# Layer-1 source lists ranked forward, four of them cut before the last group, one set of operations a destination block

## The chip, the cores and the metric

The kernel runs on one core of one Trainium2 chip. Time is device time in microseconds (us), the median of several executions. TensorE is called PE in the profile, VectorE DVE, ScalarE ACT, GpSimd POOL, and SyncE, which starts plain transfers, SP. POOL starts the gathers (indirect transfers).

## The reference, cut to what matters

A graph of N = 2708 nodes with 256 features passes two layers, each followed by a residual sum and a normalisation.

```python
# layer 0: adj without its diagonal; three attention heads and two gated cells
x = layernorm(x + L0(x, adj))
# layer 1: attention over the edges with adj > 0.5, four heads of 64 channels
h = (x @ W).reshape(n, 4, 64)
e = leaky_relu(s_src[:, None, :] + s_dst[None, :, :], 0.2)
e = where((adj > 0.5)[:, :, None], e, -1e9)
alpha = softmax(e, axis=0)                        # over sources i
out = einsum('ijh,ihc->jhc', alpha, h).reshape(n, 256) + bias
x = layernorm(x + out)
```

The graph is sparse, and low-numbered nodes have many more edges than high-numbered ones.

## The kernel before, in words

**Tiling.** The nodes are 22 tiles of 128 (the last has 20 rows), in six groups of 512 destinations; group 5 has only tiles 20 and 21, 148 nodes. Layer 0 takes the groups in the order 4, 3, 2, 1, 0, 5 (`turn`, L423). A dense pass over the transposed adjacency comes first; it leaves, for each tile of sources and block of destinations, which sources have an edge, and the adjacency of layer 1 as bit words.

**Lists.** `listed(l, batch)` (L716) turns those flags into lists of source numbers for a batch of destination blocks of layer l. It runs over five engines in turn: DVE makes flags F and a scan C; PE multiplies them with constant matrices into ranks (`rk`, one PSUM bank); DVE adds positions (`pos`, one row for each span of tiles in `spans`, L519), rounds, and builds two one-hot arrays; PE multiplies them, 22 tiles in groups of four, into `lst` (one PSUM bank); ACT copies; PE transposes; DVE writes the indices (`f_idx1` for layer 1). Layer 1 has 32 blocks (`BLOCKS1`, L53: start, width, room in tiles of 128 sources), cut into five batches, `batch1`. Rooms do not depend on the data; a list is filled up to its room.

**Layer 0 by group.** `layer0` (L1074) sums gathered columns and rows on PE; `cells_and_norm` (L1130) computes attention, two gated cells (PE products, ACT sigmoid and tanh, DVE gate operations), the normalisation, and the rows of layer 1: into DRAM table T1 go 260 words of features and exponentials a node beside its adjacency bits, into X1 the normalised rows, into Sd the destinations' values. Its POOL part sums rows into `xacc` and adds a bias, eight adds a group of four tiles. Its last PE operation is the transpose of `f_dd`, by which a group's end is read below. The lists of layer 1 are written after the last group in the program (L1279).

**Layer 1.** `work1` (L1332) cuts each block's sources into steps of at most two tiles, 56 steps in all. `fetch_h` (L1344) gathers a step's rows of T1, 128 rows of 352 words in each gather, into one of five slots (`hg_ring`, two tiles each), up to four steps ahead (`ahead1` = 5). `layer1` (L1355) has three DVE operations a step, the triple: adjacency words to a mask, the maximum of destination values S and source values into q, and q times the mask. Then PE multiplies each tile's features with q, four heads a tile, into the block's accumulator; each is two instructions in the trace. When the last block of a tile of 128 destinations is complete, `finished(b)` (L1394) copies by ACT, transposes by PE, divides, adds X1 and normalises on DVE and ACT, and stores by SP. The values S of a group, 128 x 4 x 512, come by SP from Sd (`spread_values`). S, y and the transposition's input lie in arena `big`, from its start, one after the other (L1302); layer 0 uses the same bytes earlier.

**The order.** Almost every operation is recorded and not issued at once (so nearly all profile lines read L375, `Order.issue`). `spans` (L134) says which pieces of memory an operation touches, in cells of 32 bytes of a partition; from this come the dependencies. `duration` (L180) prices each operation. A list scheduler then goes forward and backward 12 times, takes the order with the shortest planned time and issues all engines' operations in it; each engine executes its own share in that order and waits only for what an operation depends on. A table `SOONER` (L85, empty) adds to the priority of all operations recorded under a named part in the first turn.

Of the kernel before, what the change touches and what calls it, by code (L numbers as in the profile page):

```python
# [84 lines left out]
SOONER = {}  # L85


class Order:
# [44 lines left out]
    @staticmethod  # L133
    def spans(ap):  # L134

        name, pat, wide = ap.tensor.name, [tuple(d) for d in ap.ap], _width(ap.dtype)
        if name.startswith("in_"):
            return name, []
        space = str(ap.space)
        if "PSUM" in space:  # L140
            return name, [(0, 1)]
        if "DRAM" in space:
            at, cell = ap.offset, 1024
        else:
            step = pat[0][0]
            at, cell = (ap.offset % step if step else ap.offset), 32
            pat = pat[1:]
        run, outer = 1, []
        for s, n in sorted((abs(s), n) for s, n in pat if s and n > 1):
            if s <= run + cell // wide:  # L150
                run = s * (n - 1) + run
            else:
                outer.append((s, n))
        starts = [at]
        for s, n in outer:
            starts = [a + k * s for a in starts for k in range(n)]
        out = []
        for a in sorted(starts):
            lo, hi = a * wide // cell, (a + run) * wide - 1
            hi = hi // cell + 1  # L160
            if out and lo <= out[-1][1]:
                out[-1] = (out[-1][0], max(hi, out[-1][1]))
            else:
                out.append((lo, hi))
        return name, out
# [234 lines left out]
def fast_path(ctx: ExitStack, tc: tile.TileContext, i: dict, out: bass.AP, bad: bass.AP):  # L400
# [22 lines left out]
    turn = [4, 3, 2, 1, 0, 5]  # L423
    ADD, SUB, MUL, MAX = ALU.add, ALU.subtract, ALU.mult, ALU.max
# [94 lines left out]
    spans = sorted({(b[2], NB) for b in BLOCKS0} | {(0, NB)})  # L519
# [3 lines left out]
    for n, (lo, hi) in enumerate(spans):  # L523
        V.tensor_scalar(pos[:, n], pos_i, float(-P * lo), None, op0=ADD)
        if lo:
            V.memset(pos[:, n, :lo], 1.0e6)
        V.tensor_add(pos[:, n, last:], pos[:, n, last:], past)
# [51 lines left out]
    batch1 = batches_of(BLOCKS1, [(0, N)])  # L579
    slot = ({}, {})  # L580
# [135 lines left out]
    def listed(l, batch):  # L716
# [11 lines left out]
        first = [blocks[k][2] if l == 0 else 0 for k in ns]  # L728
        for m, q in enumerate(first):
            if q:  # L730
                V.memset(F[:, m, :q], 0.0)
        V.tensor_tensor_scan(
# [22 lines left out]
        while m < n:  # L755
            e = m
            while e < n and first[e] == first[m]:
                e += 1
            V.tensor_add(
                r[:, m:e], ru[:, m:e],  # L760
                pos[:, spans.index((first[m], NB))].unsqueeze(1).to_broadcast([P, e - m, NB]),
            )
            m = e
# [22 lines left out]
        b_lo = min(first)  # L786
# [492 lines left out]
    for b in batch1:  # L1279
        listed(1, b)  # L1280
# [20 lines left out]
    big.reset()  # L1301
    S_ring = Ring([big.take([P, HEADS1, CH]) for _ in range(3)])  # L1302
    y_ring = Ring([big.take([P, D]) for _ in range(4)])
    o_ring = Ring([big.take([C65, HEADS1, P]) for _ in range(2)])
# [22 lines left out]
    hg_ring = Ring([lists.take([P, 2, TW1]) for _ in range(5)])  # L1327
    q_ring = Ring([lists.take([P, 2, HEADS1, P]) for _ in range(3)])
    mask_ring = Ring([lists.take([P, 2, 8, 16], U16) for _ in range(3)])
# [3 lines left out]
    for n, (d0, w, room_) in enumerate(BLOCKS1):  # L1333
        work1 += [(n, list(range(t, min(t + 2, room_)))) for t in range(0, room_, 2)]
# [9 lines left out]
    def fetch_h(j):  # L1344
        n, ts = work1[j]
        hg = hg_ring.next()
        for m, t in enumerate(ts):
            c = column[1][n] + t
            gathered(hg[:, m, :].bitcast(U32), T1, idx[1][:, c : c + 1], 0)
        hg_of[j] = hg  # L1350

    outs = {}
    x1b_of = {}

    def layer1(j):  # L1355
# [3 lines left out]
        nt, at = len(ts), d0 - base[d0 // CH]  # L1359
# [5 lines left out]
            mask, words.unsqueeze(3).to_broadcast([P, nt, nw, 16]) if nt > 1 else  # L1365
            words.unsqueeze(3).to_broadcast([P, nt, nw, 16]),
# [10 lines left out]
        if d0 % P == 0 and ts[0] == 0:  # L1377
            outs[b] = acc.next()
            x1b_of[b] = xb_ring.next()
            Q.dma_start(x1b_of[b][: size[b]], X1[b * P : b * P + size[b], :])  # L1380
        o = outs[b]
        p0 = d0 % P
        for m, t in enumerate(ts):
            with R.together():
                for h in range(HEADS1):
                    T.matmul(
                        o[:C65, h * P + p0 : h * P + p0 + w], lhsT=hg[:, m, h * C65 : (h + 1) * C65],
                        rhs=q[:, m, h, :], start=(p0 == 0 and t == 0 and h == 0), stop=(t == room_ - 1),
                        skip_group_check=True,
                    )  # L1390
        if ts[-1] == room_ - 1 and d0 + w == min((b + 1) * P, N):
            finished(b)

    def finished(b):  # L1394
# [6 lines left out]
        with R.together():  # L1401
# [6 lines left out]
        V.tensor_mul(  # L1408
            y.rearrange("p (h c) -> p h c", h=HEADS1), got[:, :, :C1], dn.unsqueeze(2).to_broadcast([p, HEADS1, C1])
        )  # L1410
# [9 lines left out]
    ahead1 = 5  # L1420
# [466 lines left out]
```

## Time and profile before

| what | us |
|---|---|
| median of three runs (lowest, highest) | 898.7 (895.02, 906.93) |
| profiled execution, its time | 901.63 |
| its span | 899.9 |
| PE busy, DVE busy | 678.9, 551.1 |
| POOL busy, ACT busy | 436.2, 233.0 |
| end of group 4, 3, 2 (last transpose of each) | 316.14, 420.00, 523.41 |
| end of group 1, 0, 5 | 615.03, 681.37, 712.44 |
| first gather of layer 1 starts | 714.55 |
| first DVE operation of layer 1 | 727.14 |

The mean granted PE clock is 0.851 of full speed. The profile is one execution, so its durations are compared with its own time; the median of the runs is 0.3% lower. Busy time is a sum over the whole span, in which different engines set the pace at different times; the ends of groups above show where one stage gives way to the next. In rows of groups, "idle before" names what ended the engine's wait.

### The profile page before, as it was taken

The page shows a single profiled execution, that of the slowest core. Times are in us where ns is not written, and L with a number is a line of the kernel's source. Part 1 is how long each engine was busy: PE and PEld are TensorE (multiplying, and loading weights), DVE is VectorE, ACT ScalarE, POOL GpSimd, SP SyncE. Part 2 cuts the span into 40 slices and gives each one's busy share as a digit, 9 for nine tenths or more (in the row PEclk, how much of TensorE's full clock was granted, in tenths as well). Part 3 has the DMA queues.
Part 4 walks back from the last instruction along what each step waited for, and adds up shares of the span by engine and source line. Part 5 has one row for each costly group of instructions (what it writes and reads, how often), then busy time and mean ns, then how long its engine had stood idle before and what let it go on. Part 6 is the DMA issues. An engine that isn't in the chain of part 4 may idle for free. (4 is left out here: it accounts for less than half of the span.)

```text
span 899.9 us, 12878 instructions
## 1 busy us (share of the span) xinstructions
PE 678.9 (75%) x4588; PEld 481.8 (54%) x4588; DVE 551.1 (61%) x1355; ACT 233.0 (26%) x496; POOL 436.2 (48%) x565
## 2 busy tenths in 40 slices
PE   1474764778769899988898879999988565776664
PEld 1463653565335555565555545564467464765553
DVE  7373576695126847763436644561498734977996
ACT  4403664001011321122111121123125301113244
POOL 7006000476725716666677777550005266777830
PEclk9995555588979999999999999999999855787886
DMA  9934886572101312243223222121004244555541
GB/s 300 335 124 144 280 307 186 164 227 59 23 17 47 120 57 51 44 113 84 51 53 91 81 74 74 51 74 42 1 1 130 106 124 124 175 154 169 159 139 47
DMA packets 60647, 103.50 MB, mean 115 GB/s; under 512 B 20887, under 2 KB 37027, under 8 KB 59935
## 3 DMA queue, kind: packets, MB, share of 16 engines
q1 hardware_dynamic: 40337, 61.41, 20.5%
q0 software_dynamic: 17472, 41.15, 17.6%
q8 instruction: 38, 0.62, 0.3%
q10 hardware_dynamic: 2766, 0.04, 0.2%
q14 instruction: 34, 0.28, 0.1%
HBM read 93.07 MB, written 12.27 MB: 117 GB/s over the span
## 5 line engine op out<-in xcount | busy, mean ns | idle before, releaser
L375 POOL DMA_INDIRECT f_raw<-in_adjT_dram,f_idx x115 | 116.2, 1011 | 47.7 <-issue 31.9
L375 PE MATMUL acc<-f_lists 128*65 128x128 f32 (+3 forms) x768 | 100.3, 303 | 51.7 <-DVE f_lists L375 37.9
L375 POOL DMA_INDIRECT f_lists<-f_T,f_idx x96 | 108.6, 1132 | 50.2 <-issue 20.6
L375 PE MATMUL side<-f_xT,f_wts 128*128 128x512 f32 (+1 forms) x288 | 123.0, 553 | 13.0 <-DVE f_big L375 11.9
L375 PE MATMUL side<-f_big,f_wts 128*128 128x512 f32 (+1 forms) x288 | 123.1, 553 | 9.5 <-ACT f_big L375 8.4
L375 PEld LDWEIGHTS acc<-f_lists 128*65 128x65 f32 x768 | 92.0, 189 | 58.4 <-DVE f_lists L375 42.6
L375 PEld LDWEIGHTS side<-f_big,f_wts 128*128 128x128 f32 x288 | 53.1, 194 | 64.4 <-issue 54.9
L375 POOL DMA_INDIRECT f_xg__133<-f_T,f_idx x36 | 39.1, 1085 | 99.5 <-DMA f_T<-f_E 71.6
L375 PEld LDWEIGHTS side<-f_xT,f_wts 128*128 128x128 f32 x288 | 51.0, 191 | 60.7 <-issue 43.3
L375 ACT ACTIVATE f_big<-f_wts 128x1024 fp8e4<-128x1024 f32 (+2 forms) x66 | 61.7, 952 | 48.3 <-DMA f_wts<-in_adjT_dram 39.8
L375 POOL TENSOR_TENSOR f_xacc<-f_xacc,f_low 128x256 f32<-128x256 f32 (+1 forms) x22 | 22.6, 1029 | 96.9 <-ACT f_low L375 96.1
L375 ACT ACTIVATE f_big<-side,f_biases 128x512 f32<-128x512 f32 (+1 forms) x48 | 30.4, 636 | 129.3 <-PE side L375 76.6
L375 DVE TENSOR_TENSOR f_big<-f_big 128x512 f32<-128x512 f32 (+1 forms) x48 | 30.4, 636 | 49.7 <-ACT f_big L375 42.8
L375 DVE TENSOR_SCALAR f_wts<-f_wts 128x1024 fp8e4<-128x1024 f32 (+1 forms) x66 | 43.2, 662 | 25.1 <-DMA f_wts<-in_adjT_dram 23.3
L375 PE MATMUL side<-f_big,f_gat_w 128*128 128x512 f32 (+1 forms) x144 | 56.1, 544 | 2.5 <-DVE f_s_d L375 1.6
L375 DVE TENSOR_TENSOR f_lists<-f_big,f_lists 128x512 f32<-128x512 f32 (+4 forms) x56 | 44.3, 791 | 21.3 <-PE acc L375 6.9
L375 PEld LDWEIGHTS <-f_big 128*128 128x128 fp8e4 x968 | 36.4, 103 | 34.2 <-issue 18.6
L375 POOL DMA_INDIRECT f_xg__135<-f_T,f_idx x33 | 34.7, 1052 | 36.9 <-PE acc L375 24.4
L375 PE MATMUL side<-f_pow,f_wts 128*128 128x8 bf16 x484 | 23.6, 170 | 37.1 <-DVE f_wts L375 35.6
L375 PEld LDWEIGHTS <-f_lists 128*32 128x32 f16 (+6 forms) x617 | 35.4, 134 | 27.1 <-DVE f_lists L375 17.2
L375 PE MATMUL lst<-f_lists 128*128 128x256 f16 (+4 forms) x285 | 37.5, 297 | 16.0 <-DVE f_lists L375 16.0
L375 DVE TENSOR_TENSOR f_lists<-f_iota,f_lists 128x2816 f16<-128x2816 f16 (+5 forms) x26 | 49.4, 1922 | 0.3
(244 smaller groups left out, 1208.2 us busy)
## 6 DMA issues: line engine op xcount, KB each, us to landing
f_wts<-in_adjT_dram SPq DMA_DIRECT2D x42, 512.0 KB
f_wts<-in_adjT_dram SPq DMA_DIRECT2D x21, 330.0 KB
f_big<-f_Rd SPq DMA_DIRECT2D x5, 1024.0 KB
f_big<-f_Sd SPq DMA_DIRECT2D x5, 1024.0 KB
f_T<-f_ah SPq DMA_DIRECT2D x21, 132.0 KB
f_X<-f_low SPq DMA_DIRECT2D x21, 128.0 KB
f_low<-f_X SPq DMA_DIRECT2D x21, 128.0 KB
out_dram<-f_big SPq DMA_DIRECT2D x21, 128.0 KB
```

The lines of the kernel that those rows point to most:

```text
L375: getattr(getattr(self.nc, engine_), method)(*args, **kw)
```

## The change

Lists: the batches of layer 1 are recorded as part `lists1`, which gets 300 more in the scheduler's first turn. For the first four blocks (`split1`, destinations 0 to 191) the lists hold only sources of tiles 0 to 19 (`SPLIT` = 20): the flags beyond are set to zero, positions come from a span (0, 20), and their gathers name T1's first 2560 rows only. The sources of tiles 20 and 21 are added as whole tiles: `hlast` is filled by two plain SP transfers and a POOL memset once, and each of the four blocks takes a further step over these two tiles, after the four blocks' listed steps.

Steps: a step holds up to five tiles, so one block is one step, but for the block of seven tiles (4 + 3); 37 steps in all. The ring of rows has three slots of five tiles, the masks have two slots, q has two slots in xT, whose columns 0 to 2559 layer 0 no longer reads once group 0 is done. Rows are fetched two steps ahead (`ahead1` = 3). Accumulation starts and stops by a count of steps left for a tile (`todo1`).

Places: S, y and the transposition's input get fixed places in `big`, each over a layer-0 buffer that is done with early. In `finished`, an even tile's division is four ACT operations in place of one DVE operation. The scheduler's cells are 16 bytes. Rooms, and so the number of gathers (96), are unchanged.

```diff
-SOONER = {}
+SOONER = {'lists1': 300}
...
             step = pat[0][0]
-            at, cell = (ap.offset % step if step else ap.offset), 32
+            at, cell = (ap.offset % step if step else ap.offset), 16
             pat = pat[1:]
...
     turn = [4, 3, 2, 1, 0, 5]
+    SPLIT = base[turn[-1]] // P
     ADD, SUB, MUL, MAX = ALU.add, ALU.subtract, ALU.mult, ALU.max
...
     G.iota(pos_i, pattern=[[P, NB]], base=0, channel_multiplier=1)
-    spans = sorted({(b[2], NB) for b in BLOCKS0} | {(0, NB)})
+    spans = sorted({(b[2], NB) for b in BLOCKS0} | {(0, NB), (0, SPLIT)})
     pos = home("f_pos", [P, len(spans), NB])
...
             V.memset(pos[:, n, :lo], 1.0e6)
-        V.tensor_add(pos[:, n, last:], pos[:, n, last:], past)
+        if hi < NB:
+            V.memset(pos[:, n, hi:], 1.0e6)
+        else:
+            V.tensor_add(pos[:, n, last:], pos[:, n, last:], past)
     ids = home("f_ids", [P, NB, NL], F16)
...
     batch1 = batches_of(BLOCKS1, [(0, N)])
+
+    split1 = range(4)
     slot = ({}, {})
...
         V.tensor_scalar(F, source[:, s0 : s0 + n, :], 0.0, None, op0=ALU.is_gt)
-        first = [blocks[k][2] if l == 0 else 0 for k in ns]
-        for m, q in enumerate(first):
+        reach = [(blocks[k][2], NB) if l == 0 else (0, SPLIT if k in split1 else NB) for k in ns]
+        for m, (q, e) in enumerate(reach):
             if q:
                 V.memset(F[:, m, :q], 0.0)
+            if e < NB:
+                V.memset(F[:, m, e:], 0.0)
         V.tensor_tensor_scan(
...
             e = m
-            while e < n and first[e] == first[m]:
+            while e < n and reach[e] == reach[m]:
                 e += 1
...
                 r[:, m:e], ru[:, m:e],
-                pos[:, spans.index((first[m], NB))].unsqueeze(1).to_broadcast([P, e - m, NB]),
+                pos[:, spans.index(reach[m])].unsqueeze(1).to_broadcast([P, e - m, NB]),
             )
...
         )
-        b_lo = min(first)
+        b_lo = min(q for q, _ in reach)
         for b0 in range(b_lo, NB, 4):
...
         cells_and_norm(g)
-    for b in batch1:
-        listed(1, b)
+    with R.part("lists1"):
+        for b in batch1:
+            listed(1, b)
...
     V.memset(inv_n, 1.0 / N)
-    big.reset()
-    S_ring = Ring([big.take([P, HEADS1, CH]) for _ in range(3)])
-    y_ring = Ring([big.take([P, D]) for _ in range(4)])
-    o_ring = Ring([big.take([C65, HEADS1, P]) for _ in range(2)])
+    most = 5
+    o_ring = Ring([big.take([C65, HEADS1, P], at=4096 + n * 2048) for n in range(2)])
+    S_ring = Ring([big.take([P, HEADS1, CH], at=a) for a in (40960, 12288, 28672)])
+    y_ring = Ring([big.take([P, D], at=24576 + n * 1024) for n in range(4)])
+    q_ring = Ring([
+        xT[:, k, : most * HEADS1 * P].rearrange("p (t h i) -> p t h i", t=most, h=HEADS1) for k in range(KD)
+    ])
     hm = home("f_hm", [C65, HEADS1])
...
     lists.reset()
-    hg_ring = Ring([lists.take([P, 2, TW1]) for _ in range(5)])
-    q_ring = Ring([lists.take([P, 2, HEADS1, P]) for _ in range(3)])
-    mask_ring = Ring([lists.take([P, 2, 8, 16], U16) for _ in range(3)])
+    hg_ring = Ring([lists.take([P, most, TW1]) for _ in range(3)])
+    mask_ring = Ring([lists.take([P, most, 8, 16], U16) for _ in range(2)])
+    hlast = lists.take([P, NB - SPLIT, TW1])
     xb_ring = Ring([low_.take([P, D], at=n * 1024) for n in range(6, 12)])
...
     for n, (d0, w, room_) in enumerate(BLOCKS1):
-        work1 += [(n, list(range(t, min(t + 2, room_)))) for t in range(0, room_, 2)]
+        step = -(-room_ // -(-room_ // most))
+        work1 += [(n, list(range(t, min(t + step, room_)))) for t in range(0, room_, step)]
+        if n == len(split1) - 1:
+            work1 += [(k, None) for k in split1]
+    todo1 = [sum(BLOCKS1[n][0] // P == b for n, _ in work1) for b in range(NB)]
     hg_of = {}
...
         n, ts = work1[j]
+        if ts is None:
+            if not last_there:
+                last_there.append(True)
+                full = NF - SPLIT
+                G.memset(hlast[:, full:], 0.0)
+                Q.dma_start(
+                    hlast[:, :full].bitcast(U32), T1[SPLIT * P : NF * P, :].rearrange("(b p) e -> p b e", p=P)
+                )
+                Q.dma_start(hlast[: size[last], full, :].bitcast(U32), T1[NF * P :, :])
+            hg_of[j] = hlast
+            return
         hg = hg_ring.next()
+        table = T1[: SPLIT * P, :] if n in split1 else T1
         for m, t in enumerate(ts):
             c = column[1][n] + t
-            gathered(hg[:, m, :].bitcast(U32), T1, idx[1][:, c : c + 1], 0)
+            gathered(hg[:, m, :].bitcast(U32), table, idx[1][:, c : c + 1], 0)
         hg_of[j] = hg
+    last_there = []
     outs = {}
...
         g, b = d0 // CH, d0 // P
-        nt, at = len(ts), d0 - base[d0 // CH]
+        nt, at = NB - SPLIT if ts is None else len(ts), d0 - base[d0 // CH]
         hg = hg_of.pop(j)
...
         V.tensor_tensor(
-            mask, words.unsqueeze(3).to_broadcast([P, nt, nw, 16]) if nt > 1 else
-            words.unsqueeze(3).to_broadcast([P, nt, nw, 16]),
+            mask, words.unsqueeze(3).to_broadcast([P, nt, nw, 16]),
             powc.unsqueeze(1).unsqueeze(1).to_broadcast([P, nt, nw, 16]), ALU.bitwise_and,
...
         )
-        if d0 % P == 0 and ts[0] == 0:
+        begin = b not in outs
+        if begin:
             outs[b] = acc.next()
...
         p0 = d0 % P
-        for m, t in enumerate(ts):
+        todo1[b] -= 1
+        for m in range(nt):
             with R.together():
...
                         o[:C65, h * P + p0 : h * P + p0 + w], lhsT=hg[:, m, h * C65 : (h + 1) * C65],
-                        rhs=q[:, m, h, :], start=(p0 == 0 and t == 0 and h == 0), stop=(t == room_ - 1),
-                        skip_group_check=True,
+                        rhs=q[:, m, h, :], start=(begin and m == 0 and h == 0),
+                        stop=(not todo1[b] and m == nt - 1), skip_group_check=True,
                     )
-        if ts[-1] == room_ - 1 and d0 + w == min((b + 1) * P, N):
+        if not todo1[b]:
             finished(b)
...
         y = y_ring.next()[:p]
-        V.tensor_mul(
-            y.rearrange("p (h c) -> p h c", h=HEADS1), got[:, :, :C1], dn.unsqueeze(2).to_broadcast([p, HEADS1, C1])
-        )
+        if b % 2:
+            V.tensor_mul(
+                y.rearrange("p (h c) -> p h c", h=HEADS1), got[:, :, :C1],
+                dn.unsqueeze(2).to_broadcast([p, HEADS1, C1]),
+            )
+        else:
+            for h in range(HEADS1):
+                S.activation(y[:, h * C1 : (h + 1) * C1], got[:, h, :C1], AF.Identity, scale=dn[:, h : h + 1])
         V.tensor_add(y, y, x1b_of.pop(b)[:p])
...
     dn_ring = Ring([home(f"f_dn{n}_", [P, HEADS1]) for n in range(2)])
-    ahead1 = 5
+    ahead1 = 3
     spread_values(0)
```

## The prediction

> **What bounds the kernel now.** I read the stretches first (busy time by engine), then the chain of waits, then POOL's timeline where layer 1 begins, then groups by form inside layer 1. Columns below: stretch and length, then busy microseconds and instructions of PE, PE load, DVE, ACT, POOL, then PE clock.
>
> ```profile
> core 0: us, PE busy (x) PEld busy (x) DVE busy (x) ACT busy (x) POOL busy (x), PEclk, DMA share, GB/s
> 250.00:640.00 390.00, 354.60 (x1295) 214.90 (x1296) 208.85 (x507) 86.40 (x195) 220.49 (x219) 0.96 0.24 65
> 640.00:683.00 43.00, 37.72 (x220) 24.84 (x219) 34.88 (x62) 12.99 (x33) 8.29 (x4) 0.96 0.00 1
> 683.00:705.00 22.00, 17.60 (x169) 16.23 (x167) 17.26 (x38) 8.76 (x20) 3.45 (x5) 1.00 0.52 169
> 705.00:719.00 14.00, 6.35 (x71) 4.78 (x72) 10.41 (x35) 5.40 (x15) 4.40 (x6) 0.79 0.31 112
> 719.00:727.00 8.00, 2.91 (x41) 2.61 (x38) 0.15 (x1) 0.26 (x1) 6.09 (x7) 0.50 0.46 130
> 727.00:750.00 23.00, 16.16 (x136) 15.33 (x136) 10.29 (x28) 0.00 (x0) 14.76 (x15) 0.50 0.44 123
> ...
> 840.00:870.00 30.00, 19.69 (x144) 17.88 (x144) 29.47 (x79) 10.90 (x33) 18.68 (x16) 0.89 0.56 157
> ```
>
> Three regimes. To 683 us layer 0 is bound by TensorE: 354.6 of 390 us busy, while DVE has 181 us free. From 683 to 719 the last group (148 nodes) is a latency chain. From 719 to 750 every engine waits in turn. After that DVE takes over, 29.5 of 30 us near the end. The chain shows what holds the start of layer 1:
>
> ```profile
> 677.17 3.26 DVE f_lists L375
> ...
> 696.50 3.09 DVE f_lists L375
> ...
> 714.68 2.07 DVE f_lists L375 x2
> ...
> 717.35 2.54 PE lst L375 x22
> ...
> 721.87 5.13 another core or an unknown queue
> ...
> 728.22 9.25 PE acc L375 x72
> ```
>
> The 3.1 to 3.3 us DVE operations are layer-1 list building, standing between the last groups' cells; the last batch of it precedes the first sums, and then a gather's landing. POOL says the same:
>
> ```profile
> 714.55 0.96 POOL L375 DMA_INDIRECT f_lists<-f_T,f_idx  x1 [0.31 <-issue]
> 718.45 0.95 POOL L375 DMA_INDIRECT f_lists<-f_T,f_idx  x1 [2.94 <-PE lst L375]
> 719.71 0.95 POOL L375 DMA_INDIRECT f_lists<-f_T,f_idx  x1 [0.30 <-PE lst L375]
> ```
>
> Gathers start 1.25 us apart; the first layer-1 DVE operation starts at 727.14. The forms that carry the rest of layer 1:
>
> ```profile
> L375 DVE TENSOR_TENSOR f_lists<-f_big,f_lists 128x1024 f32<-128x1024 f32 x18 | 22.0, 1222 | 3.2 <-DMA f_lists<-f_T,f_idx 1.3 <-remote 0.9 <-PE acc L375 0.6
> ...
> L375 DVE TENSOR_TENSOR f_lists<-f_big,f_lists 128x512 f32<-128x512 f32 x25 | 17.1, 685 | 11.8 <-remote 5.9 <-PE acc L375 3.2 <-DMA f_big<-f_Sd 2.0
> ```
>
> [...] 512 elements 0.69 us, 1024 elements 1.22, so not quite double. [...] here gather start to reader is 4.1 to 6.1 us, and I use the trace. [...] the trace grants 0.50 at 719–750 against 0.96 before.
>
> **Part 1: lists moved forward.** The four full list batches now stand on DVE among group 2's cells and group 1's sums; the fifth stays near group 0's norm. One batch costs DVE 9.9 us (the second, 670.6–682.6, summed over ten operations), PE 22 one-hot products at 0.117 (2.6 us) plus rank products and transposes (0.02 us each), ACT one copy. By instruction order, PE has 66 more list products and 92 more rank instructions in front of group 0's end, and half of the last group's attention (1.6 of 3.29 us) behind it: 7.7 + 1.9 − 1.6 = +8.0. Two batches leave the 640–683 stretch, where 5.3 us of PE stood idle; I give back 3. So group 0 ends at 681.4 + 5 = 686.4. DVE's 40 us and ACT's copies I cost at nothing: DVE has 181 free us under TensorE there. Without that cover they cost up to about 10 us a batch. From both sides: −5 if PE's 35 idle us in 250–640 swallow the products, +25 if DVE work is half exposed.
>
> **Part 2: last group without lists, layer 1's first blocks before it.** Before, group 0's end to the first gather was 681.4 to 714.5, 33 us. Some 8.5 us of list pieces on that chain leave (3.1 + 2.1 on DVE, the rest PE, ACT and index crossings); about 4.7 us of early layer-1 operations arrive. That is 29. The early gathers read only tiles 0–19, so need group 0's rows but not the last group's. They stand behind group 0's eight adds on POOL, which the trace of before ends 5.1 us after group 0 (686.45): 691.5, four gathers 3.75 more and about 5 to land: 700.2. DVE reaches the first early operation at about 696.6, some 10 us after group 0's end, where the gate operations around it stand in the trace of before, so everything queued behind it on DVE (the last group's remaining gate operations, hence its rows) waits 3.6 us. T1 whole: 686.4 + 29 + 3.6 = 719. The last group's two bias adds now stand behind 32 gathers, delaying its X1 rows on SP, and with them a later S load and the first outputs; those rows are wanted only at block 20's finish, so nothing, unless the S load is late (up to 5). The two whole tiles come by two SP transfers after the last T1 rows; 3 us or so, beside the first blocks' own work.
>
> **Part 3: layer 1.** Before, from the first gather: blocks 0–3 took 37 us (714.6–751.6), the 32-wide ones and 320 16.8, blocks 384–895 31.4, the rest to 884.7 84.9, tail 9.5. After: of blocks 0–3 only the whole tiles are left, 9: 3 for their landing, 5 for four triples of two tiles (0.93 twice, 1.57 twice; the eight tile-blocks are new work), 1 for what the ring kept back. DVE's triple (maximum, mask, product) has a pitch of 0.93 us at 256 elements, of which 0.33 is fixed; 19 fewer triples save 6.3 in all: six among 384–895 (31.4 − 2.0 = 29.4), ten later (3.3). In every even block one y product (0.42 us, DVE) becomes four ACT operations. [...] (an estimate; the nearest row, 65x128 with one pointer operand, takes 0.36, so 0.25 to 0.4 each). ACT is at a third there, so of the 4.2 to 4.6 us that eleven blocks take off DVE I count 2.5 as gained, bounds 0 and 4.6. The rows' ring falls from 10 tiles to 3 steps. A step's fetch is issued two steps ahead, so its cycle for two 64-wide tiles is issue 1.25, landing 5, DVE 1.6, PE 2, release 0.6, over three slots = 3.5 us against 3.2 measured per step, so +2.4 over eight blocks; for three 128-wide tiles 5.1 against DVE's 5.3, no loss. So 84.9 − 3.3 − 2.5 + 2.4 = 81.5. Tail 9.5 + 2 for ACT's longer chain. Sum 9 + 16.8 + 29.4 + 81.5 + 11.5 = 148; range −6 (landing 4) to +10 (landing 6).
>
> **Sum.** 719 + 148 = 867; +5.7 from last work to the span's end = 872.8, against 899.9. The profiled execution took 901.63, 1.7 over its span, so 874.5; the runs' median is 898.7, 0.3% below it: 872.
>
> **Rivals.** B: the lists are only half covered by TensorE, group 0 ends 25 us later instead of 5: 892. For it: two batches that fell in 640–683 held DVE at 34.9 of 43 us, and PE lists wait in order among cells. Against: DVE's free time at 250–640. C: the ring of three starves: landing of 6 us and an ordered POOL add 12 to layer 1: 884. For it: landings of 6.07 in the chain, and the slot is released only by the last of a step's products. Against: 3-tile steps fetch 384 rows at a time. D, the other side: in the TensorE-bound middle each batch's chain lies wholly on the path, because PE runs in program order and its one-hot products stop everything behind them until DVE, through its own gate operations, has finished: 9.9 + 2.6 + 1.3 + 0.4 + 1 for crossings = 15 a batch, 60 for four, 52 more than I count: 924. It decides from +27 over my count (no gain left), and makes a slower kernel from +45. Against it: the planner sees DVE's gaps, and PE is idle 35 us in all there now. E: early start doesn't happen, since gathers find their rows late: about 900. DVE's order excludes it: three early steps stand ahead of the last group's norm.
>
> **How the numbers follow.** Main 0.62, own range 856 to 882 (part 1 −5 below its +5 and part 3 −6, up to +10). B 0.17, C 0.13, D 0.08. A measurement of this kernel can tell about 2% from no change: below 880.7 is faster, above 916.7 slower. Faster: 0.57 of main and 0.02 of C, 0.59. Same: 0.05 of main, B's 0.17 and 0.11 of C, 0.33. Slower: D, 0.08. The likeliest is 872. The range, 854 to 898, leaves out D (0.08), main below 854 (0.06) and B above 898 (0.06), 2 in 10.
>
> **What would show it.** Right: index writes of layer 1's lists before group 0's end; group 0's last transpose near 686; the first T1 gather near 691; the last T1 rows near 719; 37 triples, with 1536-element forms near 1.76 us (an estimate: 1222 plus the 531 ns between 512 and 1024); span near 873. Group 0's end beyond 700 is B, beyond 730 D; over 8 us more DVE idle time before sums, ended by gathers, is C. What makes it wrong most easily: list work that stands in front of something TensorE needs, and the order on POOL.

## The result and the profile after

The changed kernel is slower: 928.1 us, median of four runs (925.0 to 930.3), against 902.8 us for the kernel before with its fourth run counted in; the ratio is 1.0273 (95% interval 1.0228 to 1.0319). The forecast was 872. Some executions of a kernel took over 1.5% longer than its fastest one (in e1 seven of 20, by 1.7 to 2.5%); the ratios, here and below, leave these out, while the medians count all.

The profiled execution has a span of 926.6 us. First the stretches of the kernel after, cut where its groups end (stretch and length, busy time and instructions of PE, PE load, DVE, ACT, POOL, then PE clock, DMA share, GB/s):

```profile
core 0: us, PE busy (x) PEld busy (x) DVE busy (x) ACT busy (x) POOL busy (x), PEclk, DMA share, GB/s
...
298.00:396.00 98.00, 92.67 (x342) 54.34 (x342) 56.23 (x131) 22.82 (x60) 40.46 (x42) 0.98 0.21 61
396.00:541.00 145.00, 113.66 (x637) 74.45 (x635) 96.05 (x214) 22.69 (x54) 99.21 (x87) 0.89 0.25 60
541.00:648.00 107.00, 97.22 (x323) 60.47 (x321) 53.71 (x136) 19.57 (x45) 70.13 (x75) 0.97 0.26 69
648.00:708.00 60.00, 56.94 (x202) 30.35 (x201) 23.23 (x50) 18.78 (x42) 5.64 (x8) 0.97 0.01 3
708.00:730.00 22.00, 14.21 (x91) 12.96 (x90) 6.21 (x17) 5.32 (x14) 11.71 (x12) 0.79 0.80 267
...
860.00:890.00 30.00, 16.06 (x104) 15.31 (x104) 24.91 (x41) 7.17 (x24) 25.43 (x16) 0.74 0.43 124
```

Two stretches stand out. The one from group 3's end to group 2's, 396 to 541, is 145 us long, PE is idle for 31 us of it and its clock is 0.89. The like stretch of the kernel before, in the same columns, has 11 us idle:

```profile
420.00:523.00 103.00, 91.52 (x328) 58.19 (x326) 54.68 (x144) 19.65 (x41) 74.27 (x74) 0.95 0.29 74
```

And late in layer 1 no engine is full: DVE, which was at 29.5 of 30 us before, is at 24.9, POOL at 25.4.

Ends of stages, each from one profiled execution ("last rows" is the end of DVE's scaling of the last group's T1 rows):

| end of | before | forecast | after |
|---|---|---|---|
| group 4 | 316.1 | | 297.8 |
| group 3 | 420.0 | | 396.3 |
| group 2 | 523.4 | | 541.1 |
| group 1 | 615.0 | | 648.0 |
| group 0 | 681.4 | 686.4 | 707.4 |
| last rows | 712.3 | 719 | 745.5 |
| span | 899.9 | 872.8 | 926.6 |

So of the 53.8 us between forecast and result, 21.0 arise up to group 0, 5.5 in the last group (38.1 us in place of 32.6), and 27.3 behind it (181.1 in place of 153.8).

**Up to group 0.** PE's waits of the kernel after in 396 to 541 (what waited and for what; total, times, longest):

```profile
PE rk L375 <- DVE f_idx L375: 13.7, 3, 6.2
PE lst L375 <- DVE f_lists L375: 12.9, 3, 9.8
```

That is 26.6 us of waiting for list work, as the profile counts it, by the engine that sets the pace of layer 0; in the like stretch before, PE has no wait for list work. The longest, in PE's timeline and then in DVE's (start, duration, operation, idle before it):

```profile
442.81 0.87 PE L375 MATMUL acc<-f_four__138,f_xg__135 128*128 128x208 f32 x4
453.44 4.74 PE L375 MATMUL lst<-f_lists 128*128 128x256 f16 x22 [9.76 <-DVE f_lists L375]
```

```profile
436.40 0.31 DVE L375 TENSOR_TENSOR f_four__139<-f_four__139,f_xg__136 128x156 f32<-128x156 f32 x1
444.76 0.41 DVE L375 TENSOR_TENSOR f_lists<-rk,f_pos 128x132 f32<-128x132 f32 x2 [8.04 <-PE acc L375]
...
447.02 4.82 DVE L375 TENSOR_TENSOR f_lists<-f_iota,f_lists 128x2816 f16<-128x2816 f16 x2
451.76 1.61 DVE L375 TENSOR_TENSOR f_lists<-f_lists,f_ids 128x2816 f16<-128x2816 f16 x1
```

DVE stands still for 8.0 us before it turns the ranks into lists. The view puts the end of that wait down to PE's sums, which end at 443.7; the rank products that DVE's operation reads stand at 435.8 in PE's timeline, ahead of these sums, and what held DVE until 444.76 no view shows. Then PE stands still for 9.8 us: the one-hot products come next in its fixed order, and they need the 8.6 us of list work that DVE does from 444.76 on. What follows there in PE's order, gate products at 458.01, needs no list, and yet could not start. The ends of PE's products are modelled, so the wait can be shorter than 9.8 us; ACT, which reads products that PE's timeline ends at 439.9, goes on only at 447.6.

**Layer 1.** The chain of the kernel after from 787 to 824 now has gathers' landings among DVE's long operations:

```profile
787.90 2.82 DVE f_xT L375
...
791.85 5.11 DMA f_lists<-f_T,f_idx
...
797.25 2.29 DVE f_xT L375
...
800.66 5.11 DMA f_lists<-f_T,f_idx
...
817.95 6.46 DMA f_lists<-f_T,f_idx
```

And POOL's timeline beside DVE's of the same moment:

```profile
775.93 1.41 POOL L375 DMA_INDIRECT f_lists<-f_T,f_idx  x1 [0.71 <-PE side L375]
777.64 3.19 POOL L375 DMA_INDIRECT f_lists<-f_T,f_idx  x1 [0.30 <-issue]
781.13 3.29 POOL L375 DMA_INDIRECT f_lists<-f_T,f_idx  x1 [0.30 <-issue]
784.72 0.95 POOL L375 DMA_INDIRECT f_lists<-f_T,f_idx  x1 [0.30 <-issue]
...
787.22 0.94 POOL L375 DMA_INDIRECT f_lists<-f_T,f_idx  x1 [0.30 <-issue]
788.47 3.08 POOL L375 DMA_INDIRECT f_lists<-f_T,f_idx  x1 [0.30 <-issue]
```

```profile
775.56 0.96 DVE L375 TENSOR_TENSOR f_xT<-f_xT,f_lists 128x768 f32<-128x768 f32 x1
...
777.18 2.82 DVE L375 TENSOR_TENSOR f_xT<-f_big,f_lists 128x2560 f32<-128x2560 f32 x1
779.92 0.82 DVE L375 TENSOR_TENSOR f_lists<-f_lists,f_powc 128x640 uint16<-128x640 uint16 x1
780.77 2.82 DVE L375 TENSOR_TENSOR f_xT<-f_xT,f_lists 128x2560 f32<-128x2560 f32 x1
```

The gather at 777.64 ends at 780.83, 0.83 us after the maximum has ended at 780.00; the one at 781.13 ends at 784.42, 0.83 us after the product has (783.59). The next, beside no operation of this kind, takes 0.95. Short operations do it too: the gather at 775.93 ends at 777.34, 0.82 us after an operation of 768 elements (776.52). Of the 96 gathers of layer 1 in this trace, 40 take more than 1.0 us, and every one of them ends 0.81 to 0.83 us after the end of a DVE operation with both inputs in SBUF, of 128 to 2560 elements; the kernel before has 48 such gathers and e1 26, all at 0.81 to 0.84 us. Beside DVE operations with one input, or with an input in PSUM, gathers of the kernel after take 0.94 or 0.95. In this trace no gather that has begun is held: the maximum that begins at 787.90 leaves the one of 787.22 at 0.94 us, and the next, 0.57 us into that maximum, takes 3.08. So the times fit an issue that waits for the end of the operation: the longer the operation, the longer it can wait. What is held, no run here shows. The prediction took 0.95 us a gather (1.25 from one to the next) as a constant. Over the layer, POOL's row for gathers, before and then after:

```profile
L375 POOL DMA_INDIRECT f_lists<-f_T,f_idx x96 | 108.6, 1132 | 50.2 <-issue 20.6 <-PE acc L375 11.8 <-PE side L375 3.9
```

```profile
L375 POOL DMA_INDIRECT f_lists<-f_T,f_idx x96 | 125.8, 1310 | 52.6 <-PE acc L375 24.5 <-issue 20.3 <-DMA f_X<-f_low 4.5
```

DVE's wait for gathers before, and its two largest waits after:

```profile
DVE f_lists L375 <- DMA f_lists<-f_T,f_idx: 10.2, 8, 3.0
```

```profile
DVE f_xT L375 <- DMA f_lists<-f_T,f_idx: 24.3, 11, 4.3
DVE f_xT L375 <- PE acc L375: 10.9, 8, 3.0
```

So a gather takes 1310 ns in place of 1132 on average, and DVE waits 14 us more for gathers. What DVE saves in fixed parts it gives to waiting.

### The profile page after: what moved, and what is told of

The parts are those of the page before. It is cut to its first block, busy times and chain, and to the rows that moved or that the text cites. A ratio compares the mean times of both kernels' runs of the same rounds, so it can differ in the third digit from the quotient of the medians.

```text
span 926.6 us, 12948 instructions
## 1 busy us (share of the span) xinstructions
PE 698.6 (75%) x4652; PEld 494.7 (53%) x4652; DVE 541.6 (58%) x1295; ACT 236.6 (26%) x538; POOL 462.1 (50%) x566
## 5 line engine op out<-in xcount | busy, mean ns | idle before, releaser
L375 POOL DMA_INDIRECT f_lists<-f_T,f_idx x96 | 125.8, 1310 | 52.6 <-PE acc L375 24.5
L375 POOL DMA_INDIRECT f_raw<-in_adjT_dram,f_idx x115 | 123.3, 1072 | 35.7 <-issue 32.2
L375 PE MATMUL acc<-f_xT,f_lists 128*65 128x128 f32 (+3 forms) x832 | 104.8, 304 | 43.9 <-DVE f_xT L375 38.3
L375 PE MATMUL side<-f_xT,f_wts 128*128 128x512 f32 (+1 forms) x288 | 127.7, 571 | 7.1 <-issue 4.5
L375 PE MATMUL side<-f_big,f_wts 128*128 128x512 f32 (+1 forms) x288 | 126.5, 567 | 8.4 <-ACT f_big L375 8.4
L375 PEld LDWEIGHTS acc<-f_xT,f_lists 128*65 128x65 f32 x832 | 100.3, 188 | 47.8 <-DVE f_xT L375 40.8
L375 POOL DMA_INDIRECT f_xg__133<-f_T,f_idx x36 | 37.7, 1046 | 109.0 <-DMA f_big<-in_L_gnn_a_dst_dram 52.1
L375 ACT ACTIVATE f_big<-f_wts 128x1024 fp8e4<-128x1024 f32 (+1 forms) x66 | 61.1, 952 | 50.0 <-DMA f_wts<-in_adjT_dram 33.0
L375 DVE TENSOR_TENSOR f_xT<-f_big,f_lists 128x512 f32<-128x512 f32 (+9 forms) x37 | 43.6, 1179 | 37.8 <-DMA f_lists<-f_T,f_idx 24.3
L375 PE MATMUL side<-f_big,f_gat_w 128*128 128x512 f32 (+1 forms) x144 | 59.2, 564 | 1.9 <-ACT f_ah L375 1.8
L375 PE MATMUL side<-f_pow,f_wts 128*128 128x8 bf16 x484 | 24.5, 170 | 42.9 <-DVE f_wts L375 39.5
L375 POOL DMA_INDIRECT f_ah<-in_adjT_dram,f_idx x16 | 17.5, 1092 | 65.5 <-DVE f_big L375 58.5
L375 PE MATMUL lst<-f_lists 128*128 128x256 f16 (+4 forms) x285 | 37.5, 294 | 16.0 <-DVE f_lists L375 15.7
```

The source lines that it names most:

```text
L375: getattr(getattr(self.nc, engine_), method)(*args, **kw)
```

## The experiments

Four theories. L: the forward lists make PE and DVE wait for each other in their fixed orders. S: long DVE operations hold up gathers. T, a rival of S: a step of five tiles makes TensorE wait for the whole step's product before its first tile, so the engines work in turn. R, another rival: three slots are too few. Runs came from several chips, on which the kernel before takes 843.9 to 902.8 us. So ratios to the kernel before on the same chip count; stage times of e6 to e9, e14 and e15 (one chip, 844 us before) are compared among themselves, and those of the others, whose chips differ little (895 to 903), are read against the profiles of before and after. Medians and ratios of all runs:

| run | differs from | us | ratio (95%) | gathers' mean, ns |
|---|---|---|---|---|
| changed kernel | | 928.1 | 1.0273 (1.0228–1.0319) | 1310 |
| e1 pieces | changed | 897.5 | 1.0003 (0.9975–1.0031) | 1004 |
| e10 pieces reversed | changed | 905.7 | 1.0109 (1.0064–1.0153) | 1025 |
| e13 product only | changed | 913.5 | 1.0203 (1.0151–1.0256) | 1152 |
| e3 three tiles | changed | 912.2 | 1.0213 (1.0122–1.0305) | 1174 |
| e2 not sooner | changed | 909.6 | 1.0107 (1.0020–1.0194) | 1339 |
| e4 lists alone | before | 898.2 | 1.0016 (0.9988–1.0043) | 1082 |
| e6 before in pieces | before | 842.3 | 0.9987 (0.9953–1.0020) | 1053 |
| e7 lists and pieces | before | 845.5 | 1.0041 (1.0014–1.0069) | 1042 |
| e8 pieces, no split | e1 | 847.1 | 1.0053 (1.0029–1.0077) | 1010 |
| e9 pieces, cells of 32 | e1 | 837.1 | 0.9947 (0.9921–0.9973) | 1023 |
| e11 e9, not sooner | e9 | 882.9 | 0.9843 (0.9804–0.9882) | 1046 |
| e12 e9, three tiles | e9 | 897.3 | 1.0011 (0.9977–1.0045) | 1031 |
| e14 e11, whole | e11 | 845.0 | 1.0016 (0.9992–1.0041) | 1351 |
| e15 e11, division on DVE | e11 | 828.7 | 0.9823 (0.9777–0.9869) | 1041 |

**e1: the same order, long operations in pieces.** Only the last step, the issue of the planned order, is changed, so no instruction changes its place:

```diff
             for engine_, method, args, kw in nodes[n]:
+                out_ = args[0] if args else None
+                if method in ("tensor_tensor", "tensor_mul") and engine_ == "vector" and _size(out_) > 768 and ...:
+                    for m in range(out_.shape[1]):
+                        getattr(getattr(self.nc, engine_), method)(*[a[:, m : m + 1] if isinstance(a, bass.AP) else a for a in args], **kw)
+                    continue
                 getattr(getattr(self.nc, engine_), method)(*args, **kw)
```

> The changed kernel with its order untouched; only the maximum and the product of a step with more than 768 elements are issued as one DVE operation a tile (512 or 256 elements) in place of one of up to 2560. Theory S (a gather's start on POOL is held up while a long DVE operation with two inputs in SBUF runs): gathers of layer 1 fall from 1310 ns mean to 1100-1180, the longest from 3.5 us to under 2; layer 1 from the last group's rows (745 us) to the end, 181 us, becomes 5 to 12 us shorter although DVE has some 80 more operations of 0.11 us overhead, 9 us. Rival R (the ring of three slots and the landing set the pace): gathers' mean does not matter, the end moves by 0 to +9. Layer 0 as in the changed kernel, group 0 near 707.

Measured: 1.0003, all of the loss of 0.027 gone, though DVE has 82 instructions more. From the last rows (733.5) to the span's end (892.3) it is 158.8 us, 22.3 less than in the changed kernel. POOL and DVE in e1, at the same block as above:

```profile
764.92 0.95 POOL L380 DMA_INDIRECT f_lists<-f_T,f_idx  x1 [0.30 <-issue]
766.17 0.94 POOL L380 DMA_INDIRECT f_lists<-f_T,f_idx  x1 [0.30 <-issue]
767.42 0.95 POOL L380 DMA_INDIRECT f_lists<-f_T,f_idx  x1 [0.30 <-issue]
```

```profile
764.39 3.11 DVE L378 TENSOR_TENSOR f_xT<-f_big,f_lists 128x512 f32<-128x512 f32 x5
767.42 0.85 DVE L380 TENSOR_TENSOR f_lists<-f_lists,f_powc 128x640 uint16<-128x640 uint16 x1
```

Five operations of 512 elements take 3.11 us where the one of 2560 took 2.82, and the gathers beside them are not lengthened. POOL's row and DVE's wait over e1's layer 1:

```profile
L380 POOL DMA_INDIRECT f_lists<-f_T,f_idx x96 | 96.4, 1004 | 63.8 <-PE acc L380 32.2 <-issue 16.9 <-PE side L380 4.5
```

```profile
DVE f_xT L380 <- DMA f_lists<-f_T,f_idx: 3.8, 1, 3.8
```

The gain is about twice the most that I had expected of S. Part of the reason may be T, since pieces also let TensorE begin after the first tile: its waits for DVE's products fell from 38.3 us to 15.4. e10 and e13 bear on that.

**e10: pieces from the last tile to the first**

```diff
-                    for m in range(out_.shape[1]):
+                    for m in reversed(range(out_.shape[1])):
```

> The changed kernel, order untouched, with the same pieces of one tile as the first experiment (1.0003 of before; the changed kernel 1.0273), but issued from the last tile to the first. TensorE takes the tiles from the first on, so it can start no sooner than with whole operations, while POOL's gathers find the same gaps between short operations. Theory S (gathers held up by long DVE operations): gathers' mean near 1000 ns and the ratio stays within 0.008 of 1.0003, that is 0.995 to 1.008. Theory T (TensorE waits for the whole step's product before its first tile): gathers' mean falls too, but the ratio goes back to 1.015 to 1.03. A value between divides the 0.027 between the two.

**e13: pieces for the product alone**

```diff
-                if method in ("tensor_tensor", "tensor_mul") and ...:
+                if method == "tensor_mul" and ...:
```

> The changed kernel, order untouched, with pieces in tile order for the product alone; the maximum stays one operation of up to 2560 elements. TensorE's early start is there in full, the gathers' relief by about half (mean 1120-1200 ns). Theory T: ratio 0.997 to 1.005. Theory S: half of the gain, 1.011 to 1.018.

e10: 1.0109, between the two theories; gathers 1025 ns. With TensorE's early start excluded, 0.016 of the 0.027 is still gained: that much is S. That the other 0.011 is T is not shown: TensorE's waits for DVE's products are 15.7 us in e10, where it can't start early, as much as in e1, and 25.1 in e13, where it can. e13: gathers 1152 ns, as expected, but a ratio of 1.0203, above what either theory had forecast: TensorE's early start in full and half of the gathers' relief brought only 0.007, and its interval overlaps the changed kernel's. So S is the larger part by e10, and what the rest is stays open. Behind the last rows the profiles show 164.9 us (e10) and 164.3 (e13) against 181.1 whole and 158.8 in pieces; but the profiled execution is the fastest of both (898 us, with the others at 906 to 909, in e10; 910, with the others at 912 to 919, in e13), so these two stretches flatter them.

**e3 and e12: steps of three tiles, five slots**

```diff
-    most = 5
+    most = 3
-    hg_ring = Ring([lists.take([P, most, TW1]) for _ in range(3)])
+    hg_ring = Ring([lists.take([P, most, TW1]) for _ in range(5)])
-    ahead1 = 3
+    ahead1 = 5
```

> The changed kernel with steps of at most three tiles and five slots of three (the same 15 tiles of room), rows fetched four steps ahead. DVE operations of at most 1536 elements. Theory S: only the four to seven tile steps' stalls go: gathers' mean from 1310 to about 1240 ns. Theory R (slots): DVE's waits for gathers in layer 1 fall from 24 us to under 12, and layer 1 from the last group's rows to the end from 181 to 165-172; total 910-918 with layer 0 as it is. If neither, total within 5 of 928.

> The changed kernel in pieces with cells of 32 bytes, steps of at most three tiles and five slots of three. If the ring of three slots still holds layer 1 back (POOL waits 16 us for TensorE to free slots in the parent): POOL's waits fall under 8 us, from the last group's rows to the end 143 to 149 in place of 151, ratio 0.98 to 0.99. If DVE is the bound there now: within 0.005 of 0.9947.

e3: DVE's waits for gathers fell from 24.3 to 1.5 us and the stretch behind the last rows to 167.6, but the gathers' mean fell as well (1174), as S expects of shorter operations, so it does not separate R from S. Its ratio stays at 1.0213, with an interval that reaches both the changed kernel's and 1.012, and the profiled execution (898 us) is the fastest by 13, so its stage times flatter it too. R as the cause of the loss falls by e1, which keeps three slots: there DVE's waits for gathers fall from 24.3 to 3.8 us and the loss is gone. e12, with pieces in both, brings nothing more, 1.0011 against 0.9947, but it is no clean test of slots: its DVE waits 13.1 us for S loads (2.5 in e9), and POOL 24.5 us for PE to set slots free (20.7 in e9; under 8 was expected). The rival C of the prediction saw its sign come true, over 8 us more of DVE's waiting for gathers, but not its cause: with three slots and short operations the loss is gone.

**e2, e4, e7, e11: the lists' priority**

```diff
-SOONER = {'lists1': 300}
+SOONER = {}
```

> The changed kernel without the 300 of priority for layer 1's lists; all else as changed. Theory L (the lists among the cells cost 26 us at group 0, through TensorE waiting in order for list operations of DVE [...]): waits of TensorE for list operations between groups 3 and 0 fall from 26.6 us to under 8, group 0 ends at 675-690 in place of 707, and the last group takes longer by some of the 8 to 15 us of lists that come back: total 905-920. Rival P (the delay at group 0 comes from the finer cells and the other places, that is from another order of layer 0): group 0 stays near 705, total near 928.

> The kernel before with only the lists of layer 1 ranked forward by 300. Theory L: group 0 ends 15 to 30 us later than before's 681 (TensorE's waits for list operations 15 to 27 us between groups 3 and 0); the last group without lists takes 8 to 12 less than its 31, and the first sums come without the 13 us from its end to 727: total 900-915. If the lists were covered by TensorE, as predicted: group 0 at 682-690, total 875-890.

> The kernel before with layer 1's lists ranked forward and with those 512-element pieces. The forward lists alone gave 898.2 (same as before), with group 0 at 683.7 and the last group's rows at 708.2. If the two are independent, the total moves by what the pieces alone bring: 885 to 899. Gathers' mean 1000-1050 ns.

> The changed kernel in pieces with cells of 32 bytes (0.9947 of before) without the 300 of priority for layer 1's lists. Theory L (the forward lists cost 12 to 17 us at group 0 and give 9 to 10 back behind it): group 0 ends 10 to 17 us sooner relative to group 4, the last group takes 5 to 10 longer; ratio 0.985 to 0.995. If the early start needs the lists ready at group 0: ratio above 1.00.

e4 has the priority in the kernel before, e7 also pieces of 512. e2: PE's waits for lists fell from 28.5 us to 4.8 between groups 4 and 0. What is left of them:

```profile
PE rk L375 <- DVE f_idx L375: 3.1, 1, 3.1
PE lst L375 <- DVE f_lists L375: 1.7, 2, 1.3
```

Group 0 ended at 690.3, 17 us sooner (PE busy 7.7 us less in that stretch and idle 9.6 less, since other waits take the place of some), and the ratio fell by 0.017, so L holds; theory P (finer cells or places) explains at most what is left. e4 missed both forecasts: group 0 at 683.7, which is what the prediction had said of covered lists, the last group in 24.4 us, the first layer-1 operation at 715.4 in place of 727.1, and yet no gain, 1.0016. Its profiled run was among its fastest, and there is no profile of the kernel before on its chip, so where the rest went can't be seen; PE waits 11.1 us there for list operations of DVE, against 1.5 before, between groups 4 and 0. In e7 the forward lists cost 0.005 (1.0041 against 0.9987 for e6, with intervals that just overlap), on one chip: group 0 11.9 us later, the last group 7.4 shorter. e11: 0.9843, the fastest version then; against e9 the lists' place is worth 0.010. So in no pair did forward lists gain, and they cost from nothing to 0.017, by the order that came of them.

**e6: the kernel before in pieces of 512**

> The kernel before, order untouched; the maximum and the product of a step with 1024 elements (two tiles of 128-wide blocks) are issued as two operations of 512. Theory S (long DVE operations with two SBUF inputs hold up gathers' starts): gathers' mean falls from 1132 ns to 1020-1070; DVE has 36 more operations, about 4 us, in a stage in which it is the busiest engine. Total 887 to 896 beside 894.75 for before on this chip. If the stalls matter only above 1024 elements: 896 to 900.

0.9987, no difference. Gathers became shorter (1053 ns, 1132 in the profile before), DVE got more to do, and DVE is the busiest engine there. With 1024 elements at most the stalls are not worth their cure.

**e8 and e9: the split, and the cells**

```diff
-    split1 = range(4)
+    split1 = range(0)
```

> The changed kernel in pieces (897.45) with split1 empty: lists of all blocks over all tiles, no whole tiles, so no gather before the last group's rows are there. Theory E (the early blocks lengthen the last group by as much as they save behind it): from group 0's end to the last group's rows 24 to 27 us in place of 37.3; from these rows to the end 170 to 178 in place of 158.8; total 893 to 902. If the early start pays: total 908 to 918.

> The changed kernel in pieces (897.45) with the scheduler's cells of 32 bytes again. Theory F (finer cells only free dependencies between neighbours and are worth little): total within 6 of 897. If the other order of layer 0, and with it group 0's lateness, comes from the cells: group 0 back near 683-688 from 696.2, total near 886.

e8, without the early blocks: 1.0053 against 1.0003 with them. On the chip of e8 and e9, the last group takes 26.0 us without and 34.2 with early blocks, and the stretch behind it 176.2 without and 151.3 with: 8 us lost, 25 gained. Yet group 0 ends at 641.6 in e8 and 651.7 in e9, so another order of layer 0 takes most of the difference back, and e9 has coarser cells besides. In the totals on e1's side, with cells of 16 in both, the split is worth 0.005. Theory E hit the two stages that it had forecast and the total; but the total stays near e1's since group 0 ends sooner in e8, and not, as the theory has it, since what the last group loses equals what layer 1 gains. e9's trace shows how early blocks lengthen the last group: DVE waits 3.67 us for their gather, PE 3.68 us for DVE's product, and the last group's gate products stand behind it in PE's order:

```profile
669.50 1.97 PE L380 MATMUL acc<-f_xT,f_lists 128*65 128x32 f32 x16 [3.68 <-DVE f_xT L380]
```

e9: cells of 32 gain 0.006, within what theory F allowed; with 366 us from group 4 to group 0 against 350 in e6 on the same chip, the lateness of group 0 stays.

**e14 and e15: adding up**

> The changed kernel with cells of 32 bytes and without the 300 of priority, operations whole again: the best one so far (0.9843 of before, in pieces) without its pieces. If the long operations cost what they cost in the changed kernel (0.027), whatever the order of layer 0: 1.005 to 1.014. If they cost only together with the forward lists and fine cells: 0.984 to 0.992.

> The best one so far (0.9843 of before), order untouched, with the division of the even tiles on DVE as before (one DVE operation in the place of the last of four ACT operations). By the prediction's term (2.5 us gained by leaving DVE, bounds 0 and 4.6): 0.984 to 0.990. If ACT's four operations in a row delay the end of a tile by more than DVE gains: 0.978 to 0.983.

e14: 1.0016. Whole operations cost 0.017 there, between the two forecasts. Against e15, which was on the same chip and in pieces, the stretch behind the last rows is 171.2 us against 155.3, and 16 us of 844 is 0.019: the cost is there without forward lists and fine cells, smaller than in the changed kernel. e15, with the division of even tiles back on DVE (ACT's four operations left out at the issue, one DVE operation put where the fourth was), stays within e11's interval: moving it to ACT is worth nothing that these runs can tell.

e11 and e15 beat both kernels. They are the changed kernel with its long operations in pieces, cells of 32 bytes and no priority for the lists, 1.6% and 1.8% faster than before, with intervals that end at 0.988 and 0.987: a gain, though less than the 2% that the prediction called the least that can be told from no change.

## Why the prediction was wrong

**Part 1, lists forward: the step that failed is "DVE's 40 us and ACT's copies I cost at nothing: DVE has 181 free us under TensorE there".** DVE's free time was no cover, since the list chain crosses five engines that each keep a fixed order. The 8.0 us of added PE work was about right: PE's busy time up to group 0 rose by 19.5 us (539.6 to 559.1), of which some 12 are the same matmuls taking longer (553 to 571, 553 to 567 and 544 to 564 ns in rows of 288, 288 and 144), while the granted clock was 0.89 in 396 to 541, in place of 0.95 in the like stretch before. Without lists in front (e2), group 0 ends 17 us sooner and PE waits 4.8 us for lists in place of 28.5; the forecast had put the whole of it at +5.

The lists are not all of the 26 us. The kernel after reaches group 4's end 18 us sooner than the kernel before and needs 44 us more from there to group 0's end (409.6 in place of 365.2; PE busy 27 more, idle 17 more). e2, with that same start, needs 392.3, and e11, which has cells of 32 bytes and pieces besides, needs 371.4 and reaches group 4's end at 309.2. So some 21 us more of this stretch go with another order of layer 0, of which some 11 had been gained before it; the prediction put no price on that. What of it the cells cause no run shows alone.

What the runs show is the mechanism of rival D, at some 9 of its 15 us a batch: three batches in 396 to 541 have 26.6 us of waits. I gave D 0.08, since I trusted the planner to use DVE's gaps. Group 0's end, 707.4, has the size of rival B, 25 us later, which had 0.17. And that the total of 928 is near D's 924 is luck: D puts the whole loss into layer 0, while half of it arose in layer 1. e4 shows that an end near the forecast 686.4 was possible, with another order.

**Part 2, the last group: 38.1 us in place of 32.6.** "8.5 us of list pieces leave" was near: 24.4 us in e4, 6.5 less than before. The early start's price was too low: one wait of 3.6 us. e9 shows that wait at its size on DVE (3.67 us), and PE waiting behind it. The first early operation came 15.9 us after group 0's end, 2 later than forecast, and there is one more wait which I had not counted:

```profile
720.95 8.15 another core or an unknown queue
```

This is the chain of the kernel after. In its trace no engine works from 726.99, when POOL has issued its last gather there, to 729.18; DVE is idle for 4.4 us and ACT for 8.2. The DMA share is 0.80 in 708 to 730, with 12 gathers and two S loads of 1 MB. e11 has such a wait too (5.3 us), e4, without early gathers, has none. What it waits for no view shows, so that stays open.

**Part 3, layer 1: the term that failed is "19 fewer triples save 6.3 in all".** It counted DVE's fixed part and left out what a long operation does to others: 27.3 us more than forecast behind the last rows, of which e1 gives 22.3 back without a change of order. In e1 that stretch, 158.8, lies within the range given for it (153.8 less 6, plus 10). e14 and e15 differ there by 16 us, on one chip. So the other terms of that sum were near together, and the missing one is what an operation with two SBUF inputs does to a gather (1310 ns on average in place of 1132): the term took a gather's issue as a constant. The size of an operation was right: 1536 elements measured 1.77 and 1.75 us, forecast 1.76. No run shows a loss by three slots. The 2.5 us credited for the division on ACT is not confirmed (e15), though ACT's four operations took 0.317 us each, within the 0.25 to 0.4 estimated from a row of 0.36.

**The sum.** From 0.9843 (e11), forward lists add 0.010, fine cells 0.006 (e9 to e1), long operations 0.027 (e1 to the changed kernel): 1.027. That these three add up to the measured ratio is no test, since each is a difference to the run before it in the list. In another order the shares differ: e14 gives 0.017 for long operations, e2 0.017 for forward lists. The forecast was 0.970.

## What to carry to other kernels

Before you merge small operations into long ones, look at what runs beside them: here saved fixed parts of 0.11 us an operation were outweighed by gathers of 3.3 us in place of 0.95. The 0.11 is an estimate: triples of the kernel before that stood close together started 0.94 us apart with operations of 256 elements and 1.54 with 512, so 0.34 for three operations does not grow with their size. Look at the operands too: only operations with both inputs in SBUF held gathers here; beside others they took 0.94 or 0.95 us. Work that is moved under a busy engine can make it wait, even where the engine that does most of the work has time to spare: here the list chain went to and fro between TensorE and VectorE, each with a fixed order, and both waited, in 396 to 541 TensorE 26.6 us for list work and VectorE 11.6 us for ranks. Issue the same order with one property changed: it isolates a cause that a new schedule would blur.

## What was not expected of the hardware

A gather's issue, 0.95 us alone, ended 0.83 us after the end of a DVE operation of 2560 elements that had begun before it, twice in a row (3.19 and 3.29 us), while two gathers beside five operations of 512 elements took 0.95 and 0.94. Every gather of layer 1 over 1.0 us (40 in the kernel after, 48 before, 26 in e1, 47 in e14, 35 in e15) ended 0.81 to 0.84 us after a DVE operation with both inputs in SBUF, short ones too; in the kernel after each of the 40 had begun after that operation. One operation of 512 elements takes 0.69 us, five in a row 3.11, one of 2560 2.82, so the fixed part saved by merging five is 0.29 us in all when nothing stands between them, not the 0.44 that four times the 0.11 estimated from the triples would be. And chips ran the same kernel before in 844 to 903 us, more apart than the change under study.
